# A four-image network kernel: images 3 and 4 convolved in 4 by 4 output tiles, with other weights for the attention steps between the pieces of work

## The chip, the cores and the metric

The kernel runs on one core of one Trainium2 chip. The metric is device microseconds of one execution of the program. A time is the median of three runs; beside them one execution was profiled, and all durations, groups, waits and windows below come from that one execution.

Five engines run their own instruction queues in order: PE (TensorE, matrix products), DVE (VectorE), ACT (ScalarE), POOL (GpSimd) and SP (SyncE, which issues most of the DMAs). They wait for each other through semaphores. All data are float32.

## The reference

The input is `x`, four images of 256 channels by 64 by 64 pixels. Four layers follow each other, each of the form `x = x + layer(groupnorm(x))`:

```
def _L0_conv_ref(x, smooth_w, ...):
    xs = conv3x3(x, smooth_w) + smooth_b               # 256 -> 256 channels, padding SAME
    xs = relu(group_norm(xs, gn1_w, gn1_b))
    g_x, theta_x, phi_x = three 1x1 convolutions of xs # 256 -> 128 channels
    attn = softmax(theta_x @ phi_x, axis=-1)           # 4096 x 4096 for each image
    y = attn @ g_x
    w_y = group_norm(conv1x1(y, w_w, w_b), gn2_w, gn2_b)
    return w_y * 0.1 + xs
...
x = x + L0(gn(x)); x = x + L1(gn(x)); x = x + L2(gn(x)); x = x + L3(gn(x))
```

Layer 1 is a linear attention with RMS norms, layer 2 a 3x3 depthwise convolution whose kernels are generated from the image, followed by a generated 1x1 convolution, and layer 3 a mixture of four 1x1 convolutions. This case is about the 3x3 convolution at the head of layer 0.

## The kernel before

Images are called 1 to 4 here; the code counts `b` from 0. Channels lie on the 128 partitions, in `NH` = 2 halves.

**Two streams of work.** For each image `attend(b)` is a generator of 128 attention steps. One step issues on PE two products `pf` (phi by theta, 512 columns, L1009) for the step after it and two products `py` (L1117) of its own, on ACT the two exponentials `pr` (L1010), and on DVE one addition of 1024 elements into `tot` (L132). After every sixteenth step a short chain closes a block of 512 pixels (`ended_by_dram`). Everything else is the other stream: a `Chain` of generators, one after the other. Beside the attention of image 1 it holds scaling of weights, `filters_across` and the convolution of image 2 (`convolve_second`). Beside the attention of image 2 it holds the `tail` (layers 1 to 3 and the end of layer 0) of image 1 and the convolution of image 3 (`convolve`), beside that of image 3 the tail of image 2 and the convolution of image 4, beside that of image 4 the tail of image 3. The tail of image 4 runs alone at the end.

**What sets the order.** The order of instructions is written out by hand: each engine's queue is the order in which the Python code issues. `Chain.steps` sets how the two streams are mixed. A generator's `yield n` adds `n` times the chain's rate to a credit, and each whole unit of credit lets one attention step be issued before the chain goes on. A larger `n` or rate so puts more attention steps beside the same piece of work. `w.later(k, f)` issues `f` after `k` more attention steps; products are issued one step after the DVE work that they read, and the joining of their results one step after the products. When the chain has ended, the rest of the 128 steps is issued alone, and then `project()` of the next image, which reads the normalised convolution `big`.

**The convolution in small tiles (Winograd).** `filters` and `rows_d` in DRAM hold the transformed filters. `convolve` (images 3 and 4) makes tiles of 4 rows by 2 columns of outputs. For each of six transformed rows `a`, `down` combines image rows in `ra` and `rt`, and for each of four transformed columns `across_plain` makes one input tile `v` of 1024 elements (both channel halves), and `products` multiplies it with one filter `u` of 256 KB: four products of 512 columns (L520). `joined` adds the results into `big`, `joining` combines the six rows into four. `convolve_second` (image 2) makes tiles of 4 by 4: `normalise_planar` (L652, L654) writes the normalised image with its columns sorted by their place in a tile, `across(pair)` makes two input tiles of 512 elements each for one of the pairs (1,2), (3,4), (0,5), and `products` multiplies them with two filters: eight products of 256 columns (L592). ACT and DVE combine the results by way of `sums` and write them to `outs` and `rt_outs`, column by column of a tile. `normed_relu` brings them back to the order of pixels: four activations of 256 elements (L687) where the other images have one of 1024 (L692). Eight such pieces an image; two are issued at once and six inside `project()`.

The filters' tiles `u` have three buffers. Image 2's are loaded by SP's queue, those of images 3 and 4 by ACT's queue. While the latter are loaded, the variable `turning` moves one DMA of each block of attention (`inv<-sum_d`) from ACT's queue to SP's. `copy_x` copies the image into `xs_d`, to which the convolution's result is added, in four parts of two DMAs of 512 KB.

Of the kernel before, what the change touches and what calls it, by code (L numbers as in the profile page):

```python
# [13 lines left out]
P = 128  # L14
NH = 2
HW = 64
# [82 lines left out]
def conv_preact_fast(ctx: ExitStack, tc: tile.TileContext, guard, x, wc, wtpg, ww, wqkv, wout, w1cat, wd2,  # L99
# [3 lines left out]
    nc = tc.nc  # L103
# [379 lines left out]
    def load_filter(a, k, last):  # L483

        u = filter_tile("u")
        (nc.scalar if last == 3 else nc.sync).dma_start(out=u, in_=rows_d[a, :, :, 0 if k == 0 else 2] if k in (0, last) else filters[a, :, k - 1])
        return u
# [143 lines left out]
    def input_stats():  # L631

        st = stats_tile()
        for h in range(NH):
            for c in range(8):
                nc.vector.bn_stats(st[:, h, c, :], xin[:, h, bass.ts(c, RB), :].rearrange("p y x -> p (y x)"))
                yield 0.3
        return (yield from group_finish(st, avg8, 1e-5))

    def normalise_planar(gm, rstd):  # L640

        nb = negated(gm, rstd)
        for t in (planar[:, :, 0, :], planar[:, :, HW + 1, :],
                  planar.rearrange("p h y (r i) -> p (h y) r i", r=MX)[:, :, :, IX:IX + 1]):
            nc.gpsimd.memset(t, 0.0)
        for q in range(4):
            for h in range(NH):
                rows = slice(q * HW // 4, (q + 1) * HW // 4)
                src = xin[:, h, rows, :].rearrange("p y (i r) -> p y r i", r=MX)
                to = planar[:, h, rows.start + 1:rows.stop + 1, :].rearrange("p y (r i) -> p y r i", r=MX)[:, :, :, 0:IX]  # L650
                if h == 0:
                    nc.vector.tensor_scalar(to, src, gm[:, 0:1], rstd[:, 0:1], ALU.subtract, ALU.mult)  # L652
                else:
                    nc.scalar.activation(to, src, AF.Identity, bias=nb[:, h:h + 1], scale=rstd[:, h:h + 1])  # L654
            yield 1
# [18 lines left out]
    def normed_relu(b, st, hops=0):  # L674
# [7 lines left out]
        def piece(c, h):  # L682
            cols = bass.ts(c, CH)
            if b == 1:
                tiles = bass.ts(c, IY // 4)
                for k in range(MY):
                    nc.scalar.activation(  # L687
                        image[:, h, tiles, k, :].rearrange("p i (t j) -> p i j t", j=MX),
                        outs[:, h, k].rearrange("p j (i t) -> p i j t", t=IX)[:, tiles], AF.Relu,
                        bias=sh[:, h:h + 1], scale=sc[:, h:h + 1])  # L690
            else:
                nc.scalar.activation(big[:, h, cols], big[:, h, cols], AF.Relu, bias=sh[:, h:h + 1], scale=sc[:, h:h + 1])  # L692
# [7 lines left out]
    def convolve(w, b):  # L700

        def load_filters(i):
            a, k = PRODUCTS[i]
            u = load_filter(a, k, 3)
            return lambda oh, h: u[:, h, bass.ts(oh, P)]

        turning[0] = nc.sync
        PRODUCTS = [(a, k) for a in range(TY) for k in ACROSS1]
        us = load_filters(0)
        _, gm, rstd = yield from input_stats()  # L710
        yield from normalise(gm, rstd)
        for c in (0, HW + 1):
            nc.gpsimd.memset(ra[:, :, :, c:c + 1], 0.0)
        st = stats_tile()
        products, joined, _, rows_joined, joining, stats = joiner(st, 0.5)

        rest = []

        def some(n):
            for _ in range(min(n, len(rest))):  # L720
                op, *args = rest.pop(0)
                op(*args)

        def multiply(a, k, v, u):
            ps = products(a, k, v, u)
            if k != 1:
                w.later(1, lambda: join(a, k, ps))

        def join(a, k, ps):
            dst = joined(a, k, ps)  # L730
            if k == 3 and a == 4:

                for oh in range(NH):
                    rest.extend(joining(a, oh, dst[oh]))
                for j in range(4):
                    w.later(1 + j, lambda: some(3))
                for j in range(3):
                    w.later(5 + j, lambda j=j: stats(j))
            elif k == 3 and a == 2:
                for oh in range(NH):  # L740
                    rest.extend(joining(a, oh, dst[oh]))
                for j in range(3):
                    w.later(1 + j, lambda: some(2))
            elif k == 3:
                some(len(rest))
                for oh in range(NH):
                    w.later(1, lambda oh=oh: rows_joined(a, oh, dst[oh]))

        for i, (a, k) in enumerate(PRODUCTS):
            if i % 4 == 3 and i < 16:  # L750
                copy_x(b, i // 4)
            if k == 1:
                for op, *args in down_plain(a, ra, ra):
                    op(*args)
                    yield 0.35
            v, u = across_plain(k, ra), us
            if i + 1 < len(PRODUCTS):
                us = load_filters(i + 1)
            w.later(1, lambda a=a, k=k, v=v, u=u: multiply(a, k, v, u))
            yield 0.8  # L760
        yield from w.pending()
        turning[0] = nc.scalar
        stats(3)
        yield from normed_relu(b, st, 1)

    def convolve_second(w):

# [4 lines left out]
        PRODUCTS = [(a, pair) for a in range(TY) for pair in PAIRS]  # L772
# [39 lines left out]
        def load_one(us, i, n):  # L812
            if i < len(PRODUCTS):
                a, pair = PRODUCTS[i]
                us.append(load_filter(a, pair[n], 5))

        us = []
        for n in range(2):
            load_one(us, 0, n)
        for i, (a, pair) in enumerate(PRODUCTS):  # L820
            if pair == PAIRS[0]:

                pace = 1.8 if a == 5 else 0.87
                for op, *args in down(a, planar, ra, rt, ra):
                    op(*args)
                    yield 0.75 * pace
            (v, ops), u, us = across(pair), us, []
            load_one(us, i + 1, 0)
            if i % 3 == 2 and i < 12:
                copy_x(1, i // 3)  # L830
            for op, *args in ops:
                op(*args)
                yield 0.4 * pace
            w.later(1, lambda a=a, pair=pair, v=v, u=u, after=lambda us=us, i=i: load_one(us, i + 1, 1): multiply(a, pair, v, u, after))
            yield pace
        yield from w.pending()
        stats(3)
        yield from normed_relu(1, st, 1)
# [120 lines left out]
    turning = [nc.scalar]  # L959

# [21 lines left out]
    def attend(b):  # L982
# [48 lines left out]
        def ended_by_dram(q, py, tot):  # L1031
# [10 lines left out]
            turning[0].dma_start(out=inv.rearrange("r (p k) -> r p k", k=4), in_=sum_d[at].rearrange("p (r k) -> r p k", k=4))  # L1042
# [193 lines left out]
    def linear_attention(w, b, big, qT, k4, st, sh, sums):  # L1236
# [204 lines left out]
        for c in range(NC):  # L1441
            zb = outputs(c)
            root(zb[0])
            yield 0.6
# [6 lines left out]
            yield 0.6  # L1451
# [7 lines left out]
    def generated(w, b, big, k4, st, sh, diag):  # L1459
# [40 lines left out]
        for c in range(N // 512):  # L1500
# [11 lines left out]
            yield 0.5  # L1512
# [349 lines left out]
    with tc.manual_schedule(engines={E.PE, E.Activation, E.DVE, E.Pool, E.SP}):  # L1862
        run(Chain(convolve_first).steps())
        run(project())
        for b in range(B - 1):
            attention = attend(b)
            parts = [tail(b - 1, big, qT), lambda w: convolve(w, b + 1)] if b > 0 else [
                scale_weights, filters_across, convolve_second]
            if b == 0:
                load_x(1)  # L1870
            run(Chain(both(*parts), 1.33 if b == 0 else 0.83).steps(), attention)
# [8 lines left out]
        run(Chain(tail(B - 2, big, qT, held=held), 1.2).steps(), attention)  # L1880
# [594 lines left out]
```

## Time and profile before

| what | value |
|---|---|
| median of three runs | 3016.07 us (3015.27 to 3016.13) |
| profiled execution | 3016.98 us, its span 3015.1 us |
| granted TensorE clock, mean | 0.993 |
| PE busy | 2943.2 us, 98% of the span |
| PE weight loads busy | 1493.3 us (beside PE) |
| DVE busy | 2057.8 us, 68% |
| ACT busy | 1193.7 us, 40% |
| POOL busy | 132.5 us, 4% |
| DMA | 200.54 MB, mean 67 GB/s |

The time of an execution is the span plus about 1.9 us around it. In the groups of the profile a line is read so: source line, engine, operation, output tile <- input tiles, shape and count; then busy time in all and mean nanoseconds of one; then the idle time of the engine before these instructions and what ended it. One float32 product in the code shows as two instructions on PE. Instructions of one engine can overlap at their ends, so that the busy time of a group can be less than its count times its mean.

### The profile page before, as it was taken

To read this page: it belongs to the slowest core of one execution; us is meant where nothing else is said; L and a number is where in the kernel's file an instruction comes from. 1 tells how busy PE (TensorE), PEld (TensorE's weight loads), DVE (VectorE), ACT (ScalarE), POOL (GpSimd) and SP (SyncE) were. 2 spreads that over 40 slices of the span, in tenths; PEclk is the share of its full clock that TensorE was granted. 3 is DMA by queue.
4 is the path that set the end of the run, shared out by engine and by line. 5 is a ranking of instruction groups with operands and counts; after the bars stand their busy time and mean duration, and the time that the engine had idled before them with its cause. 6 is when DMAs were issued, how large, how long until landed. Compare 5 with 4: busy or idle time off the path is not lost.

```text
span 3015.1 us, 24709 instructions
## 1 busy us (share of the span) xinstructions
PE 2943.2 (98%) x8562; PEld 1493.3 (50%) x8562; DVE 2057.8 (68%) x2835; ACT 1193.7 (40%) x2318; POOL 132.5 (4%) x182
## 2 busy tenths in 40 slices
PE   6899999999999999999999999999999999999998
PEld 3454555555565444444566444444546544444743
DVE  8737667773646994778455797578554559876584
ACT  2243433335456333323355533422435453333732
POOL 0000000001001000000011000000101100000100
PEclk9999999999999999999999999999999999999998
DMA  5245543224402225431610334243440222343011
GB/s 224 70 89 121 66 61 74 42 35 98 91 4 35 32 25 140 88 70 35 160 8 18 48 20 87 80 84 66 95 97 19 18 42 46 30 95 88 29 63 68
DMA packets 536131, 200.54 MB, mean 67 GB/s; under 512 B 471040, under 2 KB 481024, under 8 KB 532480
## 3 DMA queue, kind: packets, MB, share of 16 engines
q1 hardware_dynamic: 127808, 163.25, 17.4%
q10 hardware_dynamic: 403584, 18.88, 11.8%
q0 software_dynamic: 4608, 16.78, 3.7%
q8 instruction: 69, 1.13, 0.2%
q14 instruction: 62, 0.51, 0.1%
HBM read 130.13 MB, written 85.52 MB: 72 GB/s over the span
## 4 chain that ended last, share of the span: by engine, by line
PE 81%; DVE 12%; issue 5%; ACT 1%; POOL 0%; DMA 0%; DVEq 0%; POOLq 0%; ACTq 0%
PE pf L1009 25%; PE py L1117 24%; PE ps_conv L520 5%; PE ps_ex L1783 4%; PE ps_tp L945 4%; PE ps_qk L1291 3%; PE ps_pw L1561 3%; DVE tot L132 2%; DVE dw L135 2%; PE ps_conv L592 2%; PE ps_ctx L1318 2%; PE ps_g L950 2%; PE ps_o L1386 2%; PE ps_wy L1061 1%; PE ps_dw L1608 1%
## 5 line engine op out<-in xcount | busy, mean ns | idle before, releaser
L1010 ACT ACTIVATE pr<-pf 128x512 f32<-128x512 f32 x1024 | 603.4, 597 | 1091.6 <-PE pf L1009 1030.5
L1009 PE MATMUL pf<-tpg 128*128 128x512 f32 x2048 | 966.2, 594 | 0.0
L1117 PE MATMUL py<-pr,tpg 128*128 128x512 f32 x2048 | 961.7, 592 | 0.0
L132 DVE TENSOR_TENSOR tot<-tot,pr 128x1024 f32<-128x1024 f32 x448 | 546.0, 1219 | 180.8 <-ACT pr L1010 180.0
L1117 PEld LDWEIGHTS py<-pr,tpg 128*128 128x128 f32 x2048 | 389.1, 190 | 489.8 <-issue 481.4
L1009 PEld LDWEIGHTS pf<-tpg 128*128 128x128 f32 x2048 | 382.9, 190 | 428.5 <-issue 407.4
L135 DVE SCALAR_TENSOR_TENSOR dw<-xp,dk,dw 128x1008 f32<-128x1008 f32 x208 | 262.9, 1268 | 6.7 <-ACT dw L1553 3.7
L520 PE MATMUL ps_conv<-v,u 128*128 128x512 f32 x384 | 170.9, 593 | 3.2 <-DVE v L132 3.2
L132 DVE TENSOR_TENSOR tpg<-ps_g,bg_s 128x512 f32<-128x512 f32 x32 | 22.1, 691 | 148.7 <-PE ps_g L950 148.7
L945 PE MATMUL ps_tp<-big,wtpg_s 128*128 128x512 f32 x256 | 118.1, 603 | 5.1 <-ACT big L692 3.0
L520 PEld LDWEIGHTS ps_conv<-v,u 128*128 128x128 f32 x384 | 72.8, 190 | 95.8 <-issue 89.1
L225 POOL TENSOR_TENSOR rstd<-rstd,half 128x2 f32<-128x2 f32 x24 | 17.5, 730 | 2202.0 <-DVE rstd L373 2078.1
L1291 PE MATMUL ps_qk<-wqkv_s,xg 128*128 128x256 f32 x496 | 113.1, 379 | 0.0
L1291 PEld LDWEIGHTS ps_qk<-wqkv_s,xg 128*128 128x128 f32 x496 | 94.0, 190 | 21.3 <-issue 8.6
L1561 PE MATMUL ps_pw<-dw,pk 128*128 128x512 f32 x216 | 98.0, 593 | 0.8 <-DVE dw L135 0.8
L946 ACT ACTIVATE tpg<-ps_tp,btp_s 128x512 f32<-128x512 f32 x64 | 44.0, 687 | 97.1 <-PE ps_tp L945 97.1
L945 PEld LDWEIGHTS ps_tp<-big,wtpg_s 128*128 128x128 f32 x256 | 47.4, 193 | 57.7 <-issue 46.6
L1301 ACT ACTIVATE qk<-ps_qk,rinv 128x256 f32<-128x256 f32 x100 | 47.0, 475 | 65.0 <-PE ps_qk L1291 62.8
L950 PEld LDWEIGHTS ps_g<-wtpg_s,big 128*128 128x128 f32 x512 | 62.2, 192 | 15.3 <-issue 15.3
L132 DVE TENSOR_TENSOR v<-ra 128x1024 f32<-128x1024 f32 x58 | 69.2, 1220 | 0.3
L1791 ACT ACTIVATE res<-ps_ex,b 128x512 f32<-128x512 f32 x56 | 38.2, 687 | 78.7 <-PE ps_ex L1783 76.8
L1561 PEld LDWEIGHTS ps_pw<-dw,pk 128*128 128x128 f32 x216 | 40.9, 190 | 53.2 <-issue 49.7
(389 smaller groups left out, 3064.7 us busy)
## 6 DMA issues: line engine op xcount, KB each, us to landing
xp<-in_x_dram SPq DMA_DIRECT2D x16, 1024.0 KB, 7.4
xs_d<-big POOLq DMA_DIRECT2D x32, 512.0 KB, 6.2
wy_d<-wt SPq DMA_DIRECT2D x32, 512.0 KB, 2.8
wy<-wy_d SPq DMA_DIRECT2D x32, 512.0 KB, 4.0
out_dram<-res SPq DMA_DIRECT2D x64, 256.0 KB, 2.0
xs_d<-in_x_dram SPq DMA_DIRECT2D x24, 512.0 KB, 5.9
xs<-xs_d SPq DMA_DIRECT2D x24, 512.0 KB, 4.6
wp<-in_wp_dram SPq DMA_DIRECT2D x16, 512.0 KB, 5.4
```

The costliest lines, as they stand in the source:

```text
L132: nc.vector.tensor_tensor(o, a, b, op)
L135: nc.vector.scalar_tensor_tensor(o, a, s, b, op0, op1)
L520: nc.tensor.matmul(ps[oh], u(oh, h), v[:, bass.ts(h, 512)], start=(h == 0), stop=(h == NH - 1))
L592: nc.tensor.matmul(ps[:, bass.ts(oh, IY * IX)], u[i][:, h, bass.ts(oh, P)], v[:, i, bass.ts(h, IY * IX)], start=(h == 0), stop=(h == NH - 1))
L945: nc.tensor.matmul(ps, wtpg_s[:, h, k, :], big[:, h, cols], start=(h == 0), stop=(h == NH - 1))
L950: nc.tensor.matmul(ps[:, j, :], big[:, h, bass.ts(4 * c + j, P)], wtpg_s[:, h, 2, :], start=(h == 0), stop=(h == NH - 1))
L1009: nc.tensor.matmul(pf, phi[:, bass.ts(2 * m + s, P)], theta[:, bass.ts(q, 512)], start=True, stop=True)
L1010: nc.scalar.activation(pr[:, bass.ts(s, 512)], pf, AF.Exp)
L1117: nc.tensor.matmul(py, g[:, bass.ts(2 * m + s, P)], probs[i][:, bass.ts(s, 512)], start=(m == 0 and s == 0), stop=(m == NM - 1 and s == 1))
L1291: nc.tensor.matmul(ps[:, 0:2 * HID], xg[:, h, bass.ts(j, P)], wqkv_s[:, h, 0:2 * HID], start=(h == 0), stop=(h == NH - 1))
L1561: nc.tensor.matmul(ps, pk[:, h * NH * P + oh * P:h * NH * P + (oh + 1) * P], dw[h][:, bass.ts(s, 512)], start=(h == 0), stop=(h == NH - 1))
L1783: nc.tensor.matmul(ps, wm[h][:, bass.ts(oh, P)], big[:, h, bass.ts(c, 512)], start=(h == 0), stop=(h == NH - 1))
```

## The change

`convolve` and `convolve_second` become one function `convolve(w, b, pace)` for images 2, 3 and 4, made of `convolve_second`'s body. It is called with pace 0.87 for image 2 and 0.5 for images 3 and 4. The transformed filters of all three images are loaded by SP's queue, for images 3 and 4 the first two ahead of the input's statistics. `turning` goes, and the DMA that it moved is always issued by ACT's queue. `normed_relu` uses the four short activations for the three images. Several weights of the mixing change: input statistics 0.3 to 0.2, `normalise_planar` 1 to 0.6, the factor of the last transformed row's pace, the output stage of the linear attention 0.6 to 0.5, the generated kernels' first stage 0.5 to 0.3, and the rates of the chains (1.33 to 1.37, 0.83 to 0.82, 1.2 to 1.24).

```
-    def load_filter(a, k, last):
-        u = filter_tile("u")
-        (nc.scalar if last == 3 else nc.sync).dma_start(out=u, in_=rows_d[...] if k in (0, last) else filters[a, :, k - 1])
-        return u
+    PRODUCTS = [(a, pair) for a in range(TY) for pair in PAIRS]
+    def load_filter_of(us, i, n):
+        if i < len(PRODUCTS):
+            a, pair = PRODUCTS[i]
+            k = pair[n]
+            u = filter_tile("u")
+            nc.sync.dma_start(out=u, in_=rows_d[...] if k in (0, 5) else filters[a, :, k - 1])
+            us.append(u)
...
     # input_stats
-                yield 0.3
+                yield 0.2
     # normalise_planar
-            yield 1
+            yield 0.6
     # normed_relu
-            if b == 1:
+            if b > 0:
...
-    def convolve(w, b):
-        ...
-    def convolve_second(w):
+    def convolve(w, b, pace):
+        us = []
+        if b > 1:
+            for n in range(2):
+                load_filter_of(us, 0, n)
         _, gm, rstd = yield from input_stats()
         yield from normalise_planar(gm, rstd)
...
+        if b == 1:
+            for n in range(2):
+                load_filter_of(us, 0, n)
         for i, (a, pair) in enumerate(PRODUCTS):
             if pair == PAIRS[0]:
-                pace = 1.8 if a == 5 else 0.87
+                slow = (2.07 if a == 5 else 1) * pace
                 for op, *args in down(a, planar, ra, rt, ra):
                     op(*args)
-                    yield 0.75 * pace
+                    yield 0.75 * slow
             (v, ops), u, us = across(pair), us, []
-            load_one(us, i + 1, 0)
+            load_filter_of(us, i + 1, 0)
             if i % 3 == 2 and i < 12:
-                copy_x(1, i // 3)
+                copy_x(b, i // 3)
             for op, *args in ops:
                 op(*args)
-                yield 0.4 * pace
+                yield 0.4 * slow
             w.later(1, ... multiply(a, pair, v, u, after))
-            yield pace
+            yield slow
...
-    turning = [nc.scalar]
-            turning[0].dma_start(out=inv..., in_=sum_d[at]...)
+            nc.scalar.dma_start(out=inv..., in_=sum_d[at]...)
...
     # linear_attention, output stage, twice
-            yield 0.6
+            yield 0.5
     # generated, first stage
-            yield 0.5
+            yield 0.3
...
-            parts = [tail(b - 1, big, qT), lambda w: convolve(w, b + 1)] if b > 0 else [
-                scale_weights, filters_across, convolve_second]
+            parts = [tail(b - 1, big, qT), lambda w: convolve(w, b + 1, 0.5)] if b > 0 else [
+                scale_weights, filters_across, lambda w: convolve(w, 1, 0.87)]
...
-            run(Chain(both(*parts), 1.33 if b == 0 else 0.83).steps(), attention)
+            run(Chain(both(*parts), 1.37 if b == 0 else 0.82).steps(), attention)
...
-        run(Chain(tail(B - 2, big, qT, held=held), 1.2).steps(), attention)
+        run(Chain(tail(B - 2, big, qT, held=held), 1.24).steps(), attention)
```

## The prediction, made before the changed kernel ran

> **What bounds the kernel now.** I read the page first, its shares by engine:
>
> ```profile
> PE 2943.2 (98%) x8562; PEld 1493.3 (50%) x8562; DVE 2057.8 (68%) x2835; ACT 1193.7 (40%) x2318; POOL 132.5 (4%) x182
> ```
>
> PE has no room anywhere, so work taken from PE is time won, unless an engine with less work over the whole falls behind in one stage. Next, the window of image 3's convolution (us, then busy time of PE, PEld, DVE, ACT and POOL, granted clock, DMA share, GB/s), and below it 37 us of image 2's:
>
> ```profile
> 1214.00:1409.00 195.00, 193.38 (x455) 85.64 (x454) 160.11 (x183) 51.59 (x84) 0.87 (x3) 1.00 0.33 66
> ...
> 583.00:620.00 37.00, 37.00 (x88) 16.36 (x87) 36.73 (x42) 13.14 (x22) 0.00 (x0) 1.00 0.38 21
> ```
>
> The first has 35 us of room on VectorE. The second is the form that the change gives images 3 and 4: both engines full, and PE not held, because in that stretch no product was due from VectorE's newest results. Then the chain of waits (start, duration, engine, work), for the price of a product and of `project()`:
>
> ```profile
> 334.87 3.45 PE ps_conv L592 x16
> ...
> 701.33 3.43 PE ps_tp L945 x8
> ...
> 711.57 2.55 ACT big L687 x4
> ...
> 748.49 1.72 PE pf L1009 x4
> ...
> 1245.62 3.43 PE ps_conv L520 x8
> ...
> 1427.17 3.43 PE ps_tp L945 x8
> ...
> 1471.51 1.72 PE pf L1009 x4
> ```
>
> An instruction of 512 columns takes 3.43/8 = 0.429 us of PE's time, one of 256 columns 3.45/16 = 0.216. Last, VectorE in image 2's stage (start, duration):
>
> ```profile
> 597.97 1.22 DVE L132 TENSOR_TENSOR tot<-tot,pr 128x1024 f32<-128x1024 f32 x1
> 599.11 1.22 DVE L135 SCALAR_TENSOR_TENSOR xp<-rt,xp 128x1024 f32<-128x1024 f32 x1
> ...
> 602.64 1.28 DVE L135 SCALAR_TENSOR_TENSOR ra<-big,ra 128x1088 f32<-128x1088 f32 x1
> 603.84 1.22 DVE L132 TENSOR_TENSOR tot<-tot,pr 128x1024 f32<-128x1024 f32 x1
> 604.98 2.46 DVE L583 BATCH_NORM_STATS2 st<-xp 128x6 f32<-128x512 f32 x4
> 607.36 1.21 DVE L132 TENSOR_TENSOR tot<-tot,pr 128x1024 f32<-128x1024 f32 x1
> ```
>
> An instruction of 1.22 us is followed after 1.14 when the next is queued, one of 1.28 after 1.20; four statistics take 2.38 to the next start, 0.595 each, though one lasts 0.685. Queued instructions thus overlap by about 0.083 us.
>
> **The sum, part by part.**
>
> *Products.* Per image, 24 filters with four products of 512 columns, two instructions each, are 192 x 0.429 = 82.4 us. After: 36 filters with four products of 256 columns, 288 x 0.216 = 62.1. All of it is on the path: -20.3 an image, -40.6 in all.
>
> *VectorE in the convolution.* Counted from the built programs, from the normalised image to its last statistics, an image has 68 operations of 1024 elements, 64 of 512 and four normalisations of 0.806 (L661) before; after, 26 of 1024, 24 of 1088, 136 of 512 and four normalisations of 1.214 (L652: their output is written column by column). Beside them go 30 attention steps before and 35 after, each 3.43 on PE, with an addition of 1.22 on VectorE in nearly all. VectorE after, at full durations: convolution 26 x 1.22 = 31.7, 24 x 1.283 = 30.8, 136 x 0.685 = 93.2, 4.9; 33 of the steps' additions 40.3 and block ends 9.8; together 210.7 us. All queued, with 0.083 off some 234 of them: 191.3. PE after: the steps' products 120.1, the convolution's 62.1, the statistics' 3.4: 185.6. Before, by the same count, PE 188.8 against 157.6 to 172.0; the window shows 160.1 busy on VectorE, so queued spacing is the nearer row. VectorE thus becomes the longer engine of this stage, by 5.7 to 25.1 us an image.
>
> Who waits: products are issued one step after the `v` that they read, and behind them on PE's queue stand the attention's own `pf` and `py`. Once VectorE is late by more than a step, those wait too, then ScalarE's exponentials, then the next additions. The stretch at 583 could carry a lag of some 8 us only because nothing was due; in the stage as built nearly every step has a product due, so the lag becomes a wait. I take S = 10.4 us an image as PE's loss in the stage: 5.7 from queued spacing; 2.5 at its entry, where ScalarE does its four `normalise_planar` activations in three steps (4 x 2.29 + 6 x 0.6 = 12.8 against 3 x 3.43 = 10.3); and 2.2 that the stage shows today from order, not amount (195.0 - 193.4, and 0.6 at `pm`), and which I leave in. Net of today's 2.2: +8.2 an image, +16.4. The bounds are S = 2.2, all of VectorE's excess covered by the lag that PE tolerates, and S = 25.1.
>
> [...]
>
> *`project()`.* From the first `ps_tp` to the last `pf` it takes 47.2 us for image 2 (701.33 to 748.49) and 44.3 for image 3 (1427.17 to 1471.51), since a piece needs four activations of 256 elements instead of one of 1024:
>
> ```profile
> L692 ACT ACTIVATE big<-big,sh,sc 128x1024 f32<-128x1024 f32 x24 | 29.4, 1231 | 8.3 <-DVE sh L132 8.3
> ...
> L687 ACT ACTIVATE big<-xp,sh,sc 128x256 f32<-128x256 f32 x32 | 21.2, 817 | 2.9 <-DVE sh L132 2.9
> ```
>
> The four stand on the chain at 2.55. +2.8 an image, +5.6; bounds 0 (the ScalarE work hidden) to 2 x 8 x (2.55 - 1.23) = 21, image 2's row being the nearest.
>
> *Filters.* Each loads 256 KB into one of three buffers, 36 an image instead of 24, and now from SP's queue, behind `copy_x` (512 KB each, 5.9 us to landing) and behind waits of SP on VectorE. A buffer comes free at the end of the second half of a product pair and is needed 5.15 to 6.9 us later. In image 2's stage, on the same queue, landing took 2.5, 3.1 and 6.2 us (least, median, most), with 0.3 to 0.6 to issue. The median is hidden; the worst load misses by some 1.6 us, and if all eleven tight places of an image did, 18 us. Image 2's products show no wait at all (their group has 0.0 idle), so I take 0.
>
> *`inv<-sum_d`* goes from SP's queue back to ScalarE's. It landed in 12.3 us on the one and 11.8 on the other, and ScalarE is 26% busy there: nothing; at worst its 0.5 us in the few blocks of the stage.
>
> *The weights.* Each image keeps 128 steps, so PE's work is unchanged; steps go from the linear attention's output, the generated kernels and the statistics to the convolutions. Waits of PE in those two stages are 5.6 us today (L1416 3.4, L1478 1.5, L1386 0.7). With ScalarE and VectorE work in fewer steps they may grow by half: +2.5, bounds -5.6 and +5.6. Image 2's own stage gets the lighter weights and a rate of 1.37; I book nothing for it.
>
> Sum: 3016.98 - 40.6 + 5.6 + 16.4 + 2.5 = 3000.9. The profiled execution lay 0.9 above the median of the runs, so the forecast is 3000.
>
> **The rivals.** 0.2% of the time, 6 us, is about what a measurement of this kernel can tell from no change; so 3 us an image decide.
>
> (B) *VectorE keeps up.* S stays 2.2, as in image 2's stage, where PE tolerated a lag. Then 3016.98 - 40.6 + 5.6 + 2.5 = 2984.5. For it: PE does not wait between 583 and 620. Against: the sum of VectorE's work is above PE's even at queued spacing, and its products are due step by step.
>
> (C) *VectorE is the bound at full durations, and the kernel is slower.* Place: the 15 steps in which `across` and `down` make inputs while `sums` combines the step before. Price S = 25.1: two images x (-20.3 + 2.8 + 1.2 + 22.9) = +13, so 3030. It decides from S = 18.5, where the gain is eaten; over 21.5 it is slower by more than 0.2%. For it: where an operation waits for ScalarE or for a product, its start is not queued and the 0.083 is lost. Against: the window's 160.1 before lies near the queued sum, 157.6, not near 172.0.
>
> (D) *Filters late on SP's queue.* When VectorE lags, SP's waiting DMAs lag as well, with the filters behind them. Half of the tight places at 1 us give 5 to 6 us an image: about 3012. Against: image 2's zero.
>
> That the change doesn't do what it says is excluded: the built order has 144 products of 256 columns for each of the three images.
>
> **How the numbers follow.** My forecast 0.52, spread from the queued bound without entry costs (2991) to S = 15 (3009); (B) 0.22; (C) 0.15; (D) 0.11. Faster: nearly all of the forecast, all of (B), half of (D): 0.73. Within 0.2%: the forecast's upper edge, the other half of (D), a quarter of (C): 0.15. Slower: the rest of (C) and a little of (D), 0.12. The range goes from 2980, (B) with the weights' gain, to 3022, short of (C)'s full price.
>
> **What would show it.** After: 864 instructions of 256 columns at the one product line and none of 512; 96 short activations as at L687, 12 as at L654. In image 3's stage VectorE at 97% or more with gaps on PE; "ps_conv waits for v" from 3.2 us to about 15 to 20. If that wait stays under 5, (B) holds; if it is over 40, (C). If PE or its weight loads wait for `u` on a DMA, (D). If `project()` of image 3 still takes 44 us, its term was wrong; if the stages of the tails lose more than 6 us in new waits of PE, the weights' term was.

## The result and the profile after

The changed kernel takes 3017.99 us (median of 12 runs, 3015.58 to 3022.09) beside 3016.1 for the kernel before (12 runs, 3015.27 to 3016.52): a ratio of 1.0008, 95% interval 1.0000 to 1.0017. The forecast was 3000. The profiled execution took 3020.56, 2.6 above the median (before's 0.9 above its own); its span is 3018.7 us, 3.6 more than before's, and what follows explains these 3.6.

The page's shares, and the product and activation groups (columns as before):

```profile
PE 2915.6 (97%) x8754; PEld 1533.1 (51%) x8754; DVE 2112.1 (70%) x2943; ACT 1221.3 (40%) x2366; POOL 128.6 (4%) x184
```

```profile
L596 PE MATMUL ps_conv<-v,u 128*128 128x256 f32 x864 | 202.4, 387 | 20.5 <-DVE v L132 8.1 <-issue 6.0 <-DMA u<-rows_d 3.3
...
L691 ACT ACTIVATE big<-xp,sh,sc 128x256 f32<-128x256 f32 x96 | 63.6, 818 | 8.8 <-DVE sh L132 8.8
```

PE's work fell by 27.6 us (2943.2 to 2915.6) and its idle time grew by 31.2 (71.9 to 103.1). The product group shows both: no instruction of 512 columns is left, and 20.5 us of idle time now stand before its instructions where the two old groups had 3.2. From the end of one `project()` to the start of the next lies one image's stretch of attention. That of image 2, with image 3's convolution beside it, takes 1.2 us longer than before, that of image 3 (with image 4's convolution) 1.8 less, that of image 4 1.2 less, and each of the two `project()` 2.8 more. Image 2's stretch, before and after:

```profile
753.64:1427.17 673.53, 669.58 (x1870) 329.82 (x1869) 494.21 (x657) 264.29 (x524) 27.94 (x35) 1.00 0.30 58
...
753.69:1428.42 674.73, 656.57 (x1966) 350.34 (x1965) 521.49 (x711) 270.28 (x530) 26.50 (x36) 0.99 0.33 62
```

So the 20 us taken from PE's products in each of the two convolutions came back inside the same stretch of attention.

PE's waits around image 3's convolution (total, times, longest): before, 2.2 us in all, 1.6 of it for `v` and 0.6 at `pm`; after (below the first line), from 1200 to 1430:

```profile
PE ps_conv L520 <- DVE v L132: 1.6, 1, 1.6
...
PE ps_conv L596 <- DVE v L132: 4.1, 2, 3.2
PE ps_conv L596 <- issue: 3.0, 2, 1.7
PE ps_conv L596 <- DMA u<-rows_d: 2.0, 1, 2.0
PE ps_conv L596 <- DMA u<-filters: 1.6, 1, 1.6
PE py L1051 <- ACT pr L944: 0.7, 1, 0.7
PE pm L356 <- DVE mv L132: 0.5, 1, 0.5
```

Two causes stand here. The two filter waits are the early ones. That at 1241.8 is for a load issued right behind two DMAs of `copy_x`; it took 7.0 us to land. That at 1265.9 is for a load with no copy ahead of it, which took 6.6 us beside `inv<-sum_d` (issued at 1254.7 by ScalarE, landed at 1267.7): the loads issued in that time took 4.0 to 6.6 us, those of the stage after it 2.5 to 4.2. The waits for `v` and "issue" are late ones, from 1308.9 on; in the two "issue" waits the timeline shows VectorE finishing `v` 0.1 us before PE goes on, so these too are waits for VectorE. Three windows of the stage (columns as before):

```profile
1213.00:1253.00 40.00, 37.30 (x107) 21.41 (x108) 38.59 (x48) 14.14 (x23) 0.00 (x0) 0.96 0.26 79
1253.00:1293.00 40.00, 38.42 (x133) 24.90 (x132) 32.76 (x43) 9.56 (x16) 0.00 (x0) 1.00 0.66 122
1293.00:1413.00 120.00, 112.44 (x335) 63.92 (x334) 118.83 (x154) 31.24 (x53) 0.00 (x0) 0.99 0.31 63
```

VectorE idles 7.2 us in the second window and is full in the third, where PE loses 7.6. One more reading is in the clock column: 0.96 and 0.99, where before has 1.00 from 754 to 2200 without exception. Ten us around the longest wait, and the sixteen products behind it:

```profile
1304.00:1314.00 10.00, 6.81 (x21) 4.58 (x20) 9.90 (x11) 1.19 (x2) 0.00 (x0) 0.83 0.09 28
...
1308.91 5.41 PE L596 MATMUL ps_conv<-v,u 128*128 128x256 f32 x16 [3.19 <-DVE v L132]
```

A clock of 0.83 over 10 us is 1.7 us of PE's full speed lost. It comes on top of the wait of 3.2: the clock is 1.00 up to 1308.9, and the sixteen products take 5.41 us where sixteen at 1271 take 3.62. In ten-us windows from 754 to 2200 the profiled execution loses 6.8 us in this way, by falls behind four waits (1.86, 2.04, 3.19 and 3.18 us); waits of 1.7 and less show none, and another of 1.85 none either.

### The profile page after: what moved, and what is told of

It reads as the page before. It is cut to its first block, busy times and chain, and to the rows that moved or that the text cites. A ratio compares the mean times of both kernels' runs of the same rounds, so it can differ in the third digit from the quotient of the medians.

```text
span 3018.7 us, 25384 instructions
## 1 busy us (share of the span) xinstructions
PE 2915.6 (97%) x8754; PEld 1533.1 (51%) x8754; DVE 2112.1 (70%) x2943; ACT 1221.3 (40%) x2366; POOL 128.6 (4%) x184
## 4 chain that ended last, share of the span: by engine, by line
PE 74%; DVE 16%; issue 6%; ACT 3%; DMA 1%; POOL 0%; DVEq 0%; POOLq 0%; ACTq 0%
PE pf L943 23%; PE py L1051 23%; PE ps_conv L596 4%; PE ps_ex L1717 4%; PE ps_tp L881 4%; PE ps_qk L1225 3%; DVE tot L132 3%; DVE dw L135 3%; PE ps_pw L1495 3%; PE ps_ctx L1252 2%; PE ps_dw L1542 1%; PE ps_g L886 1%; PE ps_wy L995 1%; PE ps_o L1320 1%; DVE v L135 1%
## 5 line engine op out<-in xcount | busy, mean ns | idle before, releaser
L596 PE MATMUL ps_conv<-v,u 128*128 128x256 f32 x864 | 202.4, 387 | 20.5 <-DVE v L132 8.1
L596 PEld LDWEIGHTS ps_conv<-v,u 128*128 128x128 f32 x864 | 166.5, 194 | 71.3 <-issue 32.2
L132 DVE TENSOR_TENSOR tpg<-ps_g,bg_s 128x512 f32<-128x512 f32 x32 | 22.1, 692 | 154.6 <-PE ps_g L886 154.6
L135 DVE SCALAR_TENSOR_TENSOR sums<-ps_conv,sums 128x512 f32<-128x512 f32 x72 | 49.6, 689 | 56.2 <-PE ps_conv L596 55.0
```

What stands on the lines that cost most here:

```text
L132: nc.vector.tensor_tensor(o, a, b, op)
L135: nc.vector.scalar_tensor_tensor(o, a, s, b, op0, op1)
L596: nc.tensor.matmul(ps[:, bass.ts(oh, IY * IX)], u[i][:, h, bass.ts(oh, P)], v[:, i, bass.ts(h, IY * IX)], start=(h == 0), stop=(h == NH - 1))
```

## The experiments

Four theories were set against each other. V: VectorE is the bound in the convolutions' stage. F: filters come late behind `copy_x` on SP's queue. W: the thinner weights outside the stage make new waits. C: waits cost a fall of the granted clock besides. Medians are given with the ratio to the kernel before and its 95% interval; runs made together, four at a time and at the end two, shared their runs of that kernel (3015.4 to 3016.1).

**The change in two halves.** First the new convolution with all the old weights and rates:

```
-                yield 0.2   # input statistics       +                yield 0.3
-            yield 0.6       # normalise_planar       +            yield 1
-            yield 0.5       # output stage, twice    +            yield 0.6
-            yield 0.3       # generated              +            yield 0.5
-  1.37, 0.82, 1.24          # rates                  +  1.33, 0.83, 1.2
```

> The changed kernel with the mixing weights and rates of the kernel before, so that only the convolution differs from before. Built, its convolution of image 3 goes beside steps 99 to 127 of the attention instead of 92 to 119. Theory V (VectorE is the bound in the convolutions' stage): seven steps fewer lie beside the same VectorE work, so VectorE's excess over PE at queued spacing grows by about 15 us an image and the end of the statistics has no step left to cover it; against that the 6 us of new PE waits an image outside the stage go: about 3040. Theory W (the loss comes from the thinner weights outside the convolution: waits of PE at ps_zt, ps_wy and py, about 6 us an image): 3018 - 12 = 3006. Theory F (filters late on SP's queue): no change, 3018.

Measured 3049.0, 1.0111 (1.0095 to 1.0126). V, and by more than it expected: the convolution runs into the end of the attention, and 8.8 us of wait stand before the last block's `ps_wy`, 5.0 before `ps_tp`. Part of the excess is the clock: in its profile the falls between 750 and 2210 cost 22.2 us, where the changed kernel has 6.8. The new weights are what makes the new convolution bearable.

Then the kernel before with only the new weights and rates (the same edit the other way round):

> The kernel before with only the new mixing weights and rates; convolutions unchanged. Theory W: the waits at ps_zt (3.5 us), ps_wy (0.8 more) and py (1.3) that the changed kernel shows in the tails appear here too, some 6 us an image for two images, less 1.2 in the attention of image 4: about 3027, and the granted clock falls below 1.00 around the ps_wy wait of 1.9 us. Theory V or F: the weights cost nothing by themselves, 3016.

Measured 3020.05, 1.0019 (1.0010 to 1.0028): +4.6 us, less than half of what W expected, and more than the nothing of V and F. PE's waits beside the tail of image 1 (754 to 1432) are those of the changed kernel:

```profile
PE ps_zt L1416 <- DVE z L132: 2.0, 2, 1.5
PE ps_wy L1061 <- DVE yq L132: 1.8, 1, 1.8
PE ps_zt L1416 <- DVE zr L1393: 1.5, 1, 1.5
```

Each of the two stretches is 3.7 us longer than before, that of image 4 1.2 shorter, 6.2 together in this profile (of an execution of 3024.73). The wait of 1.8 brought no fall of the clock in it.

**Filters.** `copy_x` for images 3 and 4 on ScalarE's queue:

```
-            nc.sync.dma_start(out=xs_d[b, h, :, cols], in_=...)
+            (nc.scalar if b > 1 else nc.sync).dma_start(out=xs_d[b, h, :, cols], in_=...)
```

> The changed kernel with the image's copy (eight DMAs of 512 KB an image) issued by ScalarE's queue instead of SP's for images 3 and 4, so that the filters' loads are no longer behind it. Theory F: PE's waits for filters, 3.6 us in image 3's stage and 2.7 in image 4's, vanish, and with them one fall of the granted clock (1.8 us): 3010 to 3012. Theory V: the next wait for v takes their place, within 1 us of 3018.

Measured 3018.24, 1.0009 (1.0000 to 1.0018). The waits for filters went but for 0.2 us, and yet nothing was won, for a reason that neither theory gave: a new wait of 2.9 us came, once beside each of the two convolutions. The timeline (ACTq is the queue's DMA issues):

```profile
1252.28 0.40 ACTq L976 DMA_DIRECT2D inv<-sum_d  x1
...
1252.75 12.29 ACTq L674 DMA_DIRECT2D xs_d<-in_x_dram  x2
...
1265.14 1.09 ACT L944 ACTIVATE pr<-pf 128x512 f32<-128x512 f32 x2 [11.81 <-issue]
```

Two issues took 12.29 us behind the DMA `inv<-sum_d` (14.1 us to landing), and ScalarE did no exponential for 11.81. The run didn't test F; so the copy was moved ahead on SP's own queue, one part beside each piece of `normalise_planar`:

```
-        yield from normalise_planar(gm, rstd)
+        for q, n in enumerate(normalise_planar(gm, rstd)):
+            if b > 1:
+                copy_x(b, q)
+            yield n
...
-            if i % 3 == 2 and i < 12:
+            if b == 1 and i % 3 == 2 and i < 12:
```

> The changed kernel with the image's copy for images 3 and 4 moved ahead on the same SP queue, one part beside each piece of normalise_planar, so that no filter of the convolution stands behind it; ScalarE's queue is left as it was. Theory F (late filters cost time of their own): the PE waits for filters, 2.0 + 1.6 us in image 3's stage and 1.3 + 1.4 in image 4's, go with nothing in their place, and one fall of the clock (1.7 us) with them: 3018 - 8 = 3010. Theory V (VectorE's late waits set the end of the stage): the later waits for v take over what is won, and the time stays at 3016 to 3018.

Measured 3012.63, 0.9993 (0.9983 to 1.0002): 5.4 us below the changed kernel, between the two expectations and nearer to F. Of the filters' waits 1.0 us is left in image 3's stage, for a load beside `inv<-sum_d` (6.0 us to landing), and those on VectorE stand nearly as they were:

```profile
PE ps_conv L596 <- DVE v L132: 3.5, 2, 3.2
PE ps_conv L596 <- issue: 3.0, 2, 1.7
PE ps_conv L596 <- DMA u<-rows_d: 1.0, 1, 1.0
```

A fourth buffer for `u` on top (`bufs=4`, paid with one of the four buffers of `k2`):

> The copy moved ahead (as in the run of that name, 3012.6) and a fourth buffer for the filters' tiles u; the room for it comes from the tag k2, which has three buffers instead of four. Theory F: the one wait for a filter that was left (1.0 us in image 3's stage) goes too: 3010 to 3011. Theory V: 3012 to 3013. If the third buffer of k2 was needed, the tails lose instead, to be seen after the last convolution.

Measured 3015.24, 0.9996 (0.9987 to 1.0005). No filter is waited for any more, and the late waits are the same:

```profile
PE ps_conv L596 <- DVE v L132: 4.2, 2, 3.2
PE ps_conv L596 <- issue: 3.0, 2, 1.7
```

VectorE stands idle for 5.8 us between 1213 and 1413 where the changed kernel has 9.8, and still it is late by as much at the end. The two stretches take 2.0 and 2.1 us less than with the copy alone, but in its profile PE reaches image 2's attention 2.6 us later than there, in the part where `k2` also serves the first image's convolution: most likely the price of the missing buffer, which no run tests alone.

**VectorE.** Every second operation of `down` left out for images 3 and 4:

```
-                for op, *args in down(a, planar, ra, rt, ra):
-                    op(*args)
+                for n, (op, *args) in enumerate(down(a, planar, ra, rt, ra)):
+                    b > 1 and n % 2 or op(*args)
```

> The changed kernel with 12 of the 24 operations of down left out for images 3 and 4 (every second of each list; the transformed rows are then wrong), all else in its place: VectorE has some 14 us less to do an image in the stage, PE the same. Theory V: the four late waits for v (7 us an image, three of 0.9 to 1.7 and one of 3.2) go, with the fall of the clock behind the longest: 3018 - 17 = about 3001. Theory F or W: 3018, the waits for filters and those in the tails remain.

Measured 3003.03, 0.9958 (0.9944 to 0.9972), as V expected. The page of waits has no named wait for `v` left in image 3's stage, and the clock stays at 1.00 from 754 to 2200; what heads the list is F's:

```profile
PE ps_conv L596 <- DMA u<-filters: 1.6, 1, 1.6
PE ps_conv L596 <- DMA u<-rows_d: 1.5, 1, 1.5
PE ps_conv L596 <- issue: 1.3, 1, 1.3
```

So some 14.4 us less work on VectorE an image (12 operations at the queued 1.20) brought 15 in all for the two images, about half of it back. Both mended, copy ahead and half of `down` left out:

> The copy moved ahead (3012.6) and 12 of the 24 operations of down left out for images 3 and 4 (3003; the transformed rows are then wrong). If late filters and VectorE's excess are separate losses that add up: 3003 - 5 = 2998. If they are one loss seen twice: 3002 to 3003.

Measured 3000.87, 0.9950 (0.9936 to 0.9963): 2.2 less than with `down` alone, where the copy alone had brought 5.4. The two losses add only in part; in its profile a filter is still waited for, for 1.6 us, in each of the two stages. And 3000.87 is 16 us above the 2984.5 that the sum gives without any new loss on VectorE, so V and F are not the whole of it.

Next, work taken from VectorE and given to GpSimd instead of left out:

```
-                tt(tot, tot, probs[i], ALU.add)
+                (nc.gpsimd if 0 < b < B - 1 and 92 <= i < 122 and m % 2 == 0
+                 else nc.vector).tensor_tensor(tot, tot, probs[i], ALU.add)
```

> The changed kernel with 13 of the attention's 30 additions into tot beside the convolutions of images 3 and 4 done by GpSimd instead of VectorE: VectorE has 14.8 us less to do an image. Theory V: as with half of down left out, 3003 or a little less. Rival P: GpSimd takes more than a step (3.4 us) for 1024 elements, or slows VectorE's own instructions while it runs, and VectorE waits for it before its next addition: no gain, or slower than 3018.

Measured 3031.11, 1.0053 (1.0039 to 1.0067): rival P. The group, and a piece of the timeline at the worst wait (6.3 us before `ps_conv`):

```profile
L1056 POOL TENSOR_TENSOR tot<-tot,pr 128x1024 f32<-128x1024 f32 x26 | 70.1, 2698 | 331.4 <-ACT pr L944 178.5 <-DVE tot L1056 99.0 <-DVE tot L132 37.6
```

```profile
1305.95 3.19 POOL L1056 TENSOR_TENSOR tot<-tot,pr 128x1024 f32<-128x1024 f32 x1 [12.24 <-DVE tot L1056]
1306.98 3.25 DVE L135 SCALAR_TENSOR_TENSOR xp<-xp 128x1024 f32<-128x1024 f32 x1
```

GpSimd takes 2.7 us for an addition, less than a step. But VectorE's `xp<-xp`, 1.22 us alone, takes 3.25 and ends 1.09 after GpSimd's, nearly its own length: three of them that start beside an addition take 3.33 on average. Its operations that read PSUM, `sums<-ps_conv,sums` for one, take 0.688 beside an addition and 0.687 without.

**Order inside the stage.** First, other factors for the six rows:

```
-                slow = (2.07 if a == 5 else 1) * pace
+                slow = ((0.8, 0.8, 1, 1.3, 1.05, 2.2)[a] if b > 1 else 2.07 if a == 5 else 1) * pace
```

> The changed kernel with the weights of the convolution's yields made different for the six transformed rows of images 3 and 4 (factors 0.8, 0.8, 1, 1.3, 1.05, 2.2 instead of 1, 1, 1, 1, 1, 2.07), so that about two attention steps move from the first two rows, where VectorE idles some 7 us, to the fourth to sixth, where it is full. Theory V2 (VectorE's total would nearly fit, but its work is uneven along the stage): the late waits for v fall from 7 us an image to 3 or less and the fall of the clock behind the 3.2 us wait goes: 3018 - 2 x 6 = 3006. Theory V1 (VectorE's total is the bound, wherever the steps lie): within 2 us of 3018.

Measured 3018.56, 1.0011 (1.0002 to 1.0020): nothing won. Waits of 1.3, 2.3 and 2.2 us now stand in the first two rows. The copy moved ahead was meant to free them:

> The copy moved ahead together with the factors by row (0.8, 0.8, 1, 1.3, 1.05, 2.2). Alone, the factors cut the late waits for v from 7.1 us to 3.7 in image 3's stage and won nothing, with waits of 1.3, 2.3 and 2.2 us in the first two rows, where the filters stood behind the copy. Theory V2 with F (uneven VectorE work, and filters as the second limit that hid it): with both out of the way some 3 us and a fall of the clock (1.7 us) an image go beyond the copy alone: 3012.6 - 9 = 3003. Theory V1 (VectorE's total is the bound): 3012 as with the copy alone.

Measured 3013.56, 0.9994 (0.9985 to 1.0003), as with the copy alone. The waits for `v` in image 3's stage still sum to 6.0 us, in other places (two of 2.6 and 2.7 the longest).

`ps_wy` one step later, with the copy ahead (a `yield` more between the multiplication of `yt` and the product):

> The copy moved ahead, and in each block of attention that ends by way of DRAM the product ps_wy issued one step later than the VectorE multiplication it reads. Theory C (a wait near 1.9 us costs twice: itself, and in some runs 1.7 us of granted clock): the wait of 1.85 us before ps_wy in images 2 and 3 goes, with the clock's falls behind it, which made the runs with the copy alone lie at 3011 to 3013 or at 3017 to 3019: 3012.6 - 4 = 3008 and a narrower spread. Rival: another wait on VectorE takes its place within the next steps: 3012.

Measured 3015.89, 0.9998 (0.9989 to 1.0007). The wait of 1.85 us went; `ps_pw` waits 1.4 and 0.9 us instead of 0.4, and a wait of 1.8 appears in the convolution. All four edits together:

> The copy moved ahead, the fourth buffer for u, the factors by row and ps_wy one step later, together. If filters, uneven VectorE work and the clock's falls are separate losses: 3018 - 5 - 9 - 4 = about 3000. If VectorE's total is the bound whatever else is mended: about 3010.

Measured 3018.71, 1.0011 (1.0002 to 1.0020). Each of the two stretches takes 5.0 us less than before, the best of the kernels with all their work; but PE reaches image 2's attention 5.5 us later than before in this profile, again with three buffers of `k2`.

**More steps beside the convolution.** First the output stage's weight back, which leaves two steps less:

```
-            yield 0.5
+            yield 0.6   # linear attention, output stage, twice
```

> The changed kernel with the weight of the linear attention's output stage back at 0.6 (from 0.5), the rest of the new weights kept: the convolution goes beside steps 94 to 121 instead of 92 to 119. Theory W: the waits of PE at ps_zt, 3.45 us in each of two images, go: 3018 - 7 = 3011. Theory V: two steps fewer lie beside the statistics and the end of the convolution, and what is won at ps_zt is lost there: 3016 to 3019.

Measured 3028.00, 1.0037 (1.0024 to 1.0051). Of the 3.5 us at `ps_zt` 1.5 stayed and `ps_b` waits 1.4; the stage itself got worse by more: 11.6 us of waits before `ps_conv` and one of 3.1 at its entry. Three runs free steps by other means: the statistics of the next image's input go beside the tail's last products, where VectorE is idle for 14 us:

```
+        if b + 2 < B:
+            early_st[b + 2] = stats_tile()
         for i, (c, oh) in enumerate(pieces):
...
+            if b + 2 < B:
+                h, k = divmod(i, 8)
+                nc.vector.bn_stats(early_st[b + 2][:, h, k, :], xin[:, h, bass.ts(k, RB), :]...)
             yield 0.1
```

> The copy moved ahead, and the 16 statistics of the next image's input issued beside the last products (ps_ex) of the tail, where VectorE has 14 us with nothing to do, instead of beside three attention steps of their own ahead of the convolution. The convolution starts three steps earlier (products at 89 to 117 instead of 92 to 119) with as many steps beside it as before; two to three steps more are left at its end. If VectorE's work per PE time in the stage decides: the stage itself is no lighter, 3011 to 3013. If the steps at its end were too few: 3008.

> As with the early statistics, and the convolutions of images 3 and 4 at pace 0.55 instead of 0.5: their products lie beside steps 89 to 120, three attention steps more beside the same convolution than in the changed kernel. If VectorE's work per PE time decides: each step brings 3.43 us of PE's work and 1.14 of VectorE's, so 2.3 us of relief, 7 an image: 3012.6 - 14 = 2999. If the order inside the stage decides: 3011 to 3013.

> As with the early statistics, at pace 0.6: products beside steps 90 to 123, five to six steps more than in the changed kernel, and four left at the end. If VectorE's work per PE time decides: up to 11 us an image, 2991, less what the shorter end loses (some 3 us an image): 2997. If the order inside the stage decides: 3012, or slower where the end is left bare.

Measured 3021.21 (1.0017, 1.0008 to 1.0026), 3017.19 (1.0003, 0.9994 to 1.0012) and 3041.40 (1.0084, 1.0070 to 1.0098). These are for the pace at 0.5, 0.55 and 0.6. At 0.55 the waits before `ps_conv` fell from 7.5 us (copy alone) to 5.1, but a wait of 3.1 came at the entry in all three. ScalarE's timeline at 0.55 shows it:

```profile
1199.44 6.57 ACT L660 ACTIVATE big<-xp,nb,rstd 128x1024 f32<-128x1024 f32 x3 [2.50 <-DVE nb L135]
```

Three of the four `normalise_planar` activations fell into one step, and the exponentials stood behind 6.6 us of them. At 0.6 the end is bare as well (one wait of 4.9 us before `ps_conv`, one of 4.4 before the last `ps_wy`). Two runs with the entry spread out (`normalise_planar` at 1.0 and 0.9), the freed steps used inside the convolution (pace 0.53) or in the output stage (0.6):

> The copy moved ahead, the input's statistics beside ps_ex, the weight of normalise_planar at 1.0 for images 3 and 4 and their pace at 0.53; products beside steps 91 to 120. If the entry's wait (3.1 us) and the clock's fall behind it were what hid the gain of the freed steps: 3017 - 2 x (2.4 + 1.7) and 2 us an image for the steps, about 3005. If VectorE's excess turns up as another wait wherever the steps are put: 3011 to 3015.

> As the other, but the freed steps given back to the linear attention's output stage (weight 0.6 instead of 0.5), the convolutions' pace at 0.5 and normalise_planar at 0.9; products beside steps 92 to 120, nearly as in the changed kernel. If the waits at ps_zt (3.45 us an image) were a loss by themselves: 3012.6 - 7 = 3006. If what is taken there turns up elsewhere: 3011 to 3015.

Measured 3020.87 (1.0009, 1.0000 to 1.0018) and 3014.05 (0.9989, 0.9980 to 0.9998). The second is the one version with all its work, of fifteen tried, whose interval lies below the kernel before, by 2 us; it is 4 below the changed kernel. Its stage still has waits of 2.9 at `pm`, 2.4 before `py` and 4.7 before `ps_conv`.

**The clock, from run to run (C).** The runs of one program fall into groups. With pace 0.53: three at 3010.0 to 3013.6, eight at 3020.1 to 3022.0. Its profile is of the upper group, and its windows at three waits of image 3's stage (2.6, 2.0 and 2.7 us) all have a clock of 0.83; the one at the wait of 2.0:

```profile
1304.00:1314.00 10.00, 8.03 (x24) 5.58 (x24) 9.90 (x13) 1.79 (x3) 0.00 (x0) 0.83 0.28 78
```

Five such falls cost 8.5 us of clock between 754 and 2200 there, about the distance of the two groups. The mean clock of each run says the same: 0.992 and 0.993 in the lower three, 0.989 and 0.990 in the others, and 0.003 of 3020 us is 9. The last version has three runs at 3008.8 and eight at 3013.9 to 3015.2, 5.3 apart; its profile loses 5.1. No lower run has a profile, so it is not shown that these very falls are missing there. Against it, the kernel before with the new weights has two groups as well (3019.3 to 3020.5, 3024.6 to 3025.1), and its profile, of the upper one, has no fall between 754 and 2200: where its 5 us lie is open.

## Why the prediction was wrong

**Right:** the price of products in undisturbed stretches (sixteen of 256 columns still take 3.45 us on the chain), and `project()`: +2.8 us an image, from 1428.42 to 1475.57 in the chain, 47.2. VectorE did become the longer engine of the stage, with 193.3 us of work from the normalised image to its last statistics (1205.41 to 1408.51) where the sum had 191.3. ScalarE's entry wait was small (0.7 where 2.5 was put). The check by 160.1 us on VectorE before was loose: its window is 10 us longer than the stage, which has 154.6 (1227.20 to 1411.96).

**The step that failed is S, PE's loss in the stage: it held VectorE's lateness and nothing else.** It was put at 10.4 us an image, +8.2 net of the old waits. From the profiles: image 2's stretch is +1.2 = -20.3 (products) + 3.7 (weights, by the run with these alone) + 17.8, and image 3's -1.8 = -20.3 + 3.7 + 14.8. Two images: 32.6 where the sum had 16.4. By rows of the two profiles the 32.6 is made of this:

| part, both images | us | in the sum |
|---|---|---|
| waits for VectorE and ScalarE in the stage, net of the old ones | 12.3 | 16.4 |
| waits for filters (3.6 and 2.7) | 6.3 | 0 |
| lost clock (5.1 and 1.7) | 6.8 | no term |
| PE's busy time beyond products, weights and clock (2.2 and 2.8) | 5.0 | no term |
| other waits | 2.2 | no term |

- *VectorE's term held in size.* The late waits for `v` come to 7.1 us an image, near the 5.7 that the subtraction of the two engines' sums gave. That subtraction is the least loss: it holds if VectorE is never idle, and VectorE stood idle for 9.8 us of the stage's 203.1, most of it before `sums`, for PE's products. The filters' waits are not what makes VectorE late at the end: without them (fourth buffer) the late waits are 7.2. Half of `down` left out took the late waits away (7.1 to 1.3 us in image 3's stage) and all 6.8 us of lost clock, and brought 15.0 us.
- *The filters were taken at nothing*, by image 2's row with 0.0 idle, and so was `inv<-sum_d`. Moving the copy alone brought 5.4 us for the two images, half of the rival's price; a wait beside `inv<-sum_d` stayed. Image 2's row was no neighbour: in the trace before, its products are spread over 335 us (334.7 to 669.6), those of image 3 now over 174 (1222.4 to 1396.0). Of the 2.7 us in image 4's stage the page puts 1.4 down to `tot`; that it is a filter is argued from its place, that of a filter's wait in other runs.
- *No term for the clock.* The list of bounds priced a wait at its own length. 6.8 us were lost behind four waits in the profiled execution: two for `v`, one for a filter, one at `ps_wy`.

Where PE's 5.0 us of longer busy time come from no run tests; 1.4 us more of the same kind are within the 3.7 an image of the run with the weights alone.

By the prediction's own signs: the waits for `v` with those called "issue" are 14.1 us, just short of the 15 to 20 of the forecast, so neither (B) nor (C); PE waits for `u`, the sign of (D); and the new waits in the tails are some 9 us, over the 6 that were to show the weights' term wrong.

*Full durations* (the third rival) did not decide, but have a part. In these rows of the changed kernel's stage, an operation that doesn't read the result just written still follows at queued spacing, and one that does read it loses that:

```profile
1306.84 1.29 DVE L135 SCALAR_TENSOR_TENSOR v<-ra 128x512 f32<-128x512 f32 x2
1308.16 0.69 DVE L132 TENSOR_TENSOR v<-v 128x512 f32<-128x512 f32 x1
1308.88 0.69 DVE L135 SCALAR_TENSOR_TENSOR v<-v 128x512 f32<-128x512 f32 x1
1309.49 1.22 DVE L132 TENSOR_TENSOR tot<-tot,pr 128x1024 f32<-128x1024 f32 x1
```

The two `v<-ra` take 1.29 us in all, so the second starts some 0.60 after the first (1.29 less one length of 0.69), and what follows it, which reads its result, 0.72 later. The first `v<-v`, whose result the next one reads, takes 0.72 to the next start as well; the second, followed by an addition of other tiles, 0.61. The five such pairs of `v<-v` in the stage lie 0.72 or 0.73 apart, and the two of a pair of `sums<-ps_conv,sums`, of which the second overwrites what the first reads, 0.71 to 0.73 (1.40 to 1.42 for both). An addition into `tot` is followed after 1.13 or 1.14 by a queued operation on other tiles, and after 1.25 or 1.26 by `inv<-tot`, which reads it. Full durations thus hold in this stage for neighbours that depend on each other, not for all.

**The weights** were put at +2.5 in all and cost 4.6 by themselves by the medians, 6.2 in the stretches of the profile. **The break-even** of S = 18.5 went by weights of 1.2 an image; with 3.7 it is 16.0. With 17.8 and 14.8 net of the old 2.2, S is 20.0 and 17.0, and each image lost: 4.0 and 1.0 us, less the 1.2 of image 4's attention.

What stays open: how VectorE's part divides between order and amount. With VectorE's work left whole, no edit brought PE's idle time in image 2's stretch below 15 us (18.2 in the changed kernel, 4.0 before), but the orders tried are few, and one that was not tried may do better.

## What to carry to other kernels

Where a change shifts work from the bound engine to one that then is as full, the difference of their sums is the least loss, and it is the loss by that engine alone: go through the other things that the stage now needs sooner (loads, the steps taken from elsewhere) and give each its own term, from a row of a stage that runs as fast. Price a wait of the matrix engine at itself plus a possible fall of the clock behind it: here waits of 1.9 us and more were often followed by 1.7 us of lost clock. When steps that are moved make a wait go in one place and come in another, the amount of work may be the limit; leaving work out, as with half of `down`, tests that at once. A loss that goes with nothing in its place, as the filters' did, is a loss of its own.

## What the hardware showed that was not expected

- *The clock fell after short waits.* Waits of 1.9 us and more were often followed by 1.7 us of lost clock, in some cases by 3.4, but not in every run or place: two of 2.8 and 2.9 us with the copy on ScalarE's queue by none. Waits up to 1.8 us that stand by themselves were followed by none in the profiles read by ten us from 754 to 2200 (before, after and eight of the runs). In the changed kernel a gap of 1.86 us (up to 994.99) and one of 2.04 (up to 1241.77) were enough, and one of 1.85 (up to 1722.01) was not. Why nearly the same gap cost 1.7 us in one place and nothing in another, no run here shows.
- *A GpSimd addition held VectorE up.* An operation of 1.22 us with both inputs in SBUF took 3.25 where it started beside a GpSimd addition of 3.19, ending 1.09 after it, while those with one input in PSUM stayed at 0.69.
- *A queue of DMA issues held its engine.* Two issues that take 0.6 us each on SP took 12.29 on ScalarE's queue behind `inv<-sum_d`, and ScalarE's computing stood still for 11.81. Beside the same DMA, loads on the other queue took longer too: in the changed kernel filters landed in 4.0 to 6.6 us beside it and in 2.5 to 4.2 after it, and with the copy out of the way in 5.1 to 6.9 beside it. That the DMA is the cause is likely, not tested.
